# Layer-1 attention on four 32-row strips: heads in neighbouring pairs, mask and maximum in one operation

## The chip, the cores and the metric

The kernel runs on one core of a Trainium2 chip. The metric is the device time of one execution in microseconds (us), the median of several runs; before the change it is 2142.12 us, the median of three (2135.86 to 2145.12). The profile is of one more execution. A core has TensorE (PE; its weight loads are listed apart as PEld), VectorE (DVE), ScalarE (ACT), GpSimd (POOL) and SyncE (SP, which here only issues DMAs). Matmuls write to PSUM, from which DVE and ACT read.

## What is computed

Two transformer layers over 1024 tokens of width 512. Each is an attention and a feed-forward part with modulated layer norms. The change is in the attention of the second layer (layer 1 in the code), which has 32 query heads of size 16 and 8 key and value heads; four query heads share one key head. Cut to that:

```python
qkv = x @ w_qkv.T + b_qkv
q, k, v = split(qkv)                      # 32, 8 and 8 heads of 16
q, k = apply_rope(q), apply_rope(k)
k, v = repeat(k, 4, axis=1), repeat(v, 4, axis=1)
scores = einsum('bhqd,bhkd->bhqk', q, k) / sqrt(16)
scores = where(causal, scores, -1e20)
attn = softmax(scores, axis=-1)
out = einsum('bhqk,bhkd->bhqd', attn, v)
return out @ w_o.T + b_o
```

All data are float32.

## The kernel before

The attention of layer 1 begins at L530. `kT1` holds the keys, transposed, as 128 rows for each of the 8 key heads: the 16 values of the head stand four times, at rows 0, 32, 64 and 96, and row 16 of each such strip of 32 rows is one, the other 15 are zero. The queries stand in the same way, one of the four query heads of the group on each strip, with row 16 free for the (negative) maximum of the query's scores, so that the matmul itself subtracts the maximum. Before the change there are two such query tiles, `qT1[0]` and `qT1[1]`: `par` is one on the strips of even (odd) heads and zero on the others, so that `qT1[0]` holds heads 0 and 2 with zeros on the strips of 1 and 3, and `qT1[1]` the other way round. A matmul then takes a half of 64 rows, of which one strip is not zero.

The loop over token tiles `t` (L590 on) computes q, k and v (L596), rotates them on DVE and POOL (L617 to L624), transposes q and k on PE (L636) and evicts them: k with `evict`, which alternates between ACT and DVE (L78, L80), q once on DVE with the one mask (L640) and once on ACT with the other (L643).

Then come 16 units: `Q` is the half of the queries (512), `g` the key head; units 0 to 7 are Q=0, 8 to 15 Q=1. For each unit:

- `maxima_steps` (queries on the partitions): for each 128 queries `i`, each 512 keys `c` and each `pair` of heads, two matmuls into one two-bank PSUM tile `sc` (L678), the causal mask added on the diagonal block (L685, DVE, in place), and the maximum over the keys (L688, DVE). 8 such steps for a unit of Q=0, 16 for one of Q=1.
- `maxima_rows`: the negative maximum (L702, DVE), four transposes (L705), and the result added into row 16 of both query tiles (L708, DVE, twice).
- `probs_steps` (keys on the partitions): for each block of 128 keys `kb` and each pair two matmuls (L722) into `sc`, the mask on diagonal blocks (L729, DVE), and the exponential (L733, ACT) into `pr`. 8 steps for Q=0, 16 for Q=1.
- `context`: four matmuls, one per head, that accumulate probabilities times values (L745); then `context_copy` (L754, ACT) and `normalize` (L762 transposes on PE, L765 and L766 on DVE).

The pool `sp` of `sc` tiles has three buffers, which the maxima and the probabilities share; they rotate in the order of the steps, so that a step waits until the step three before it has been read out. The other two PSUM banks are for transposes and for the context.

The order around it is written out by hand: the maxima of units 0 and 1 come first; then, for each unit `n`, its probability steps with the maxima steps of unit `n+2` spread among them. One probability step is followed by its share of maxima steps, then by `tick()`, which counts down the deferred work: the context of block `kb` is due three ticks after its second step, `maxima_rows` two ticks after a unit's end, `context_copy` four, `normalize` six; `finish_half` projects the output of a half. With one maxima step to one probability step a block of keys is queued on PE as: probabilities of pair 0, maxima of pair 0, probabilities of pair 1, maxima of pair 1, context of the block before.

## Time and profile before

| what | value |
|---|---|
| median of three runs | 2142.12 us |
| the profiled execution | 2138.97 us, of which its span is 2137.2 us |
| granted TensorE clock, mean | 0.98 |
| busy: PE, DVE, ACT, POOL | 2007.7, 1224.6, 654.5, 255.3 us |
| layer-1 attention, first maxima matmul to last context | 1612.6 to 2045 us |
| unit of Q=0, Q=0 maxima ahead (units 0 to 5) | 16.3 us |
| unit of Q=0, Q=1 maxima ahead (units 6 and 7) | 23.8 us |
| unit of Q=1, maxima ahead (units 8 to 13) | 34.0 us |
| unit of Q=1, none ahead (units 14 and 15) | 20.6 us |

How to read a profile line: the group lines name the source line, the engine, the operation, output and input by the program's names with partitions and elements, the count, then the busy time in us and the mean of one in ns, and after the second bar the idle time of the engine just before these instructions and who ended it. A line of windows gives a stretch, its length, and busy time and count for each engine, then the granted TensorE clock (1.00 is full), the DMA share and GB/s. A timeline line gives the start, the duration, the engine, the line and operation, the count merged into it, and in brackets how long the engine had been idle and who released it ("issue": nothing that the profile shows).

A float32 matmul appears as two records in the trace, each with its own weight load. The durations of matmul records include the latency of the pipeline; the starts tell the pace.

### The profile page before, as it was taken

The numbers are of one execution on the slowest core, as the hardware profiler recorded it, in microseconds if no ns is written. First come the engines' busy times: TensorE is split into PE (matmuls) and PEld (weight loads), VectorE is DVE, ScalarE is ACT, GpSimd is POOL, SyncE is SP. The second block draws the span as 40 slices with busy tenths as digits, with TensorE's granted clock in tenths as the row PEclk, the third lists the DMA queues.
The fourth block names the chain that finished last, engine by engine and source line by source line (L and its number), as shares of the span: only waits on it lengthen the run. The fifth ranks groups of instructions, "written<-read, shape, count | busy, mean of one in ns | idle before, by whom it ended". The sixth has DMA issues, their size and how long they took to land.

```text
span 2137.2 us, 20442 instructions
## 1 busy us (share of the span) xinstructions
PE 2007.7 (94%) x6628; PEld 914.3 (43%) x6628; DVE 1224.6 (57%) x2305; ACT 654.5 (31%) x1180; POOL 255.3 (12%) x231
## 2 busy tenths in 40 slices
PE   5979999999999999999997999999887899999989
PEld 3434454444544445444443333333353444333344
DVE  4666656766576675766654211112477898667433
ACT  1134424434234342443532100000021323344530
POOL 0211111111111211111102000000440000000000
PEclk8999999999999999999999999999997999999999
DMA  5344334444334444343345100000300000000011
GB/s 173 103 113 134 93 104 109 110 130 100 104 97 115 127 99 114 94 111 92 90 120 167 61 30 30 0 0 0 102 0 20 1 1 1 1 1 1 1 39 40
DMA packets 87785, 151.16 MB, mean 71 GB/s; under 512 B 20896, under 2 KB 34080, under 8 KB 87680
## 3 DMA queue, kind: packets, MB, share of 16 engines
q1 hardware_dynamic: 86800, 146.98, 25.5%
q0 software_dynamic: 880, 2.88, 0.4%
q8 instruction: 54, 0.88, 0.2%
q14 instruction: 51, 0.42, 0.1%
HBM read 72.18 MB, written 2.10 MB: 35 GB/s over the span
## 4 chain that ended last, share of the span: by engine, by line
PE 72%; DVE 12%; DMA 5%; ACT 4%; issue 3%; SPq 2%; POOL 1%; DVEq 0%; POOLq 0%; ACTq 0%
PE mm L233 12%; PE mm L363 8%; PE pgu L493 7%; PE sc L319 7%; PE mm L352 6%; PE sc L722 5%; PE sc L678 5%; PE mm L519 4%; PE ctx L745 3%; DMA os<-in_s_o_dram 2%; PE pgu L497 2%; DVE mx L688 2%; DVE nb L326 2%; SPq L343 2%; DVE pr L341 1%
## 5 line engine op out<-in xcount | busy, mean ns | idle before, releaser
L329 ACT ACTIVATE pr<-sc,nb 128x1024 f32<-128x1024 f32 (+7 forms) x256 | 187.6, 735 | 386.8 <-DVE nb L326 307.4
L233 PE MATMUL mm<-hT,wf 128*128 128x512 f32 x640 | 283.2, 596 | 5.8 <-ACT wf L250 5.8
L352 PE MATMUL mm<-pT,v 128*128 128x512 f32 x576 | 263.6, 603 | 19.9 <-DMA pT<-pr 19.1
L319 PE MATMUL sc<-kT,qT 128*128 128x512 f32 (+3 forms) x768 | 273.7, 487 | 4.5 <-ACT pr L329 4.5
L363 PE MATMUL mm<-wo,ctxT 128*128 128x512 f32 x512 | 236.0, 599 | 16.4 <-ACT ctxT L358 12.0
L733 ACT ACTIVATE pr<-sc 128x1024 f32<-128x1024 f32 (+1 forms) x192 | 153.8, 810 | 236.2 <-DVE sc L729 164.8
L319 PEld LDWEIGHTS sc<-kT,qT 128*128 128x128 f32 x768 | 139.6, 191 | 154.1 <-issue 127.5
L335 ACT ACTIVATE pr<-pr,rs 128x1024 f32<-128x1024 f32 (+7 forms) x256 | 187.2, 768 | 49.1 <-DVE rs L334 48.9
L688 DVE TENSOR_REDUCE mx<-sc 128x2 f32<-128x1024 f32 (+2 forms) x192 | 182.3, 955 | 30.1 <-PE sc L678 26.7
L341 DVE STREAM_TRANSPOSE pr<-pr 128x1024 f32<-128x1024 f32 (+7 forms) x256 | 178.2, 748 | 24.0 <-ACT pr L335 18.4
L326 DVE TENSOR_REDUCE nb<-sc 128x1 f32<-128x1024 f32 (+7 forms) x256 | 188.1, 750 | 3.6
L233 PEld LDWEIGHTS mm<-hT,wf 128*128 128x128 f32 x640 | 122.2, 192 | 156.0 <-issue 147.2
L678 PE MATMUL sc<-kT,qT 64*128 64x512 f32 (+3 forms) x768 | 168.2, 520 | 13.4 <-DVE mx L688 5.2
L722 PE MATMUL sc<-qT,kT 64*128 64x512 f32 (+3 forms) x768 | 170.6, 517 | 5.4 <-DVE mx L688 3.5
L352 PEld LDWEIGHTS mm<-pT,v 128*128 128x128 f32 x576 | 110.3, 194 | 144.9 <-issue 130.1
L493 PE MATMUL pgu<-hT,gu 128*128 128x512 f32 x352 | 162.8, 606 | 0.0
L369 POOL TENSOR_TENSOR x<-x,ot 128x512 f32<-128x512 f32 x64 | 81.4, 1271 | 676.0 <-DVE ot L368 565.7
L363 PEld LDWEIGHTS mm<-wo,ctxT 128*128 128x128 f32 x512 | 94.3, 190 | 132.3 <-issue 94.2
L334 DVE RECIPROCAL rs<-rs 128x1 f32<-128x1 f32 x256 | 37.9, 156 | 125.7 <-ACT pr L329 124.6
L722 PEld LDWEIGHTS sc<-qT,kT 64*128 64x128 f32 x768 | 66.3, 187 | 101.6 <-issue 55.3
L678 PEld LDWEIGHTS sc<-kT,qT 64*128 64x128 f32 x768 | 70.0, 194 | 91.5 <-ACT pr L733 35.4
L243 POOL TENSOR_TENSOR qT<-t,t 128x512 f32<-128x512 f32 x64 | 85.5, 1336 | 182.6 <-DVE t L242 182.6
(160 smaller groups left out, 1856.1 us busy)
## 6 DMA issues: line engine op xcount, KB each, us to landing
pT<-pr SPq DMA_DIRECT2D x128, 128.0 KB, 2.4
pT<-pr SPq DMA_DIRECT2D x128, 112.0 KB, 2.3
wm<-in_wmod_dram SPq DMA_DIRECT2D x48, 256.0 KB, 3.2
pT<-pr SPq DMA_DIRECT2D x128, 96.0 KB, 2.1
pT<-pr SPq DMA_DIRECT2D x128, 80.0 KB, 2.1
wi<-in_qw_q_dram SPq DMA_DIRECT2D x32, 256.0 KB, 2.9
ws<-in_s_q_dram SPq DMA_DIRECT2D x32, 256.0 KB, 3.6
oi<-in_qw_o_dram SPq DMA_DIRECT2D x32, 256.0 KB, 2.8
```

Of the source, the lines that this page charges most:

```text
L233: nc.tensor.matmul(ps, lhsT=wf[:, c, :], rhs=hT[half][:, c, :], start=(c == 0), stop=(c == NC - 1),)
L319: nc.tensor.matmul(ps[:, n0 : n0 + w], lhsT=qT[u.g * REP + r][:, bass.ts(u.qi, P)], rhs=kT[u.g][:, n0 : n0 + w], start=True, stop=True,)
L326: nc.vector.tensor_reduce(nb, ps[:, :nk], AX.X, ALU.max, negate=True)
L329: nc.scalar.activation(pr.rearrange("p b k i -> p k b i"), ps[:, :nk].rearrange("p (k b i) -> p k b i", b=NB, i=B), AF.Exp, bias=nb, accum ...
L335: nc.scalar.activation(pr, pr, AF.Copy, scale=rs)
L341: nc.vector.transpose(t, t)
L352: nc.tensor.matmul(ps, lhsT=vv[u.g][:, kj, :], rhs=u.pT[:, :, :, kj, :].rearrange("p a r i -> p r a i"), start=(kj == 0), stop=(kj == u.n ...
L363: nc.tensor.matmul(ps, lhsT=u.ctxT[:, r, :], rhs=wo[u.g][:, r, :], start=(r == 0), stop=(r == REP - 1),)
L493: nc.tensor.matmul(ps, lhsT=gu[:, c, m, :], rhs=hT[b][:, c, :], start=(c == 0), stop=False)
L678: nc.tensor.matmul(ps[:, j, :w], lhsT=qT1[pair][kp, u.g, bass.ts(qi, P)], rhs=kT1[kp, u.g, n0 : n0 + w], start=True, stop=True,)
L688: nc.vector.tensor_reduce(u.mx[:, i, pair::2, c], ps[:, :, :w], AX.X, ALU.max)
L722: nc.tensor.matmul(ps[:, j, :w], lhsT=kT1[kp, u.g, bass.ts(kb, P)], rhs=qT1[pair][kp, u.g, u.Q * QW + q0 : (u.Q + 1) * QW], start=True, st ...
```

## The change

The two query tiles become one, `qT1`, without `par`; its eviction goes through `evict`. A step takes two heads that stand next to each other (0 and 1, or 2 and 3), each matmul on its own strip of 32 rows, so that a pair uses strips 0 and 1 or 2 and 3. On the maxima steps whose keys reach the diagonal, two `tensor_tensor_reduce` replace mask and maximum: each adds a mask row `cwide` (zeros, and the causal mask in its last 128 columns) to one head's scores, writes the sum to a scratch tile `sm` and its maximum to `mx`. `maxima_rows` adds into one tile instead of two. The order of the queue changes: after the first probability step of a block comes a tick, then all maxima steps due in the block, then the second probability step and the second tick; the maxima steps come with pair 1 before pair 0. `context` takes the heads from their new places.

```diff
-        qT1 = [hp.tile([P, NKV, S], F32, tag=f"qT1{i}", name=f"qT1{i}") for i in range(2)]
-        par = hp.tile([P, 2], F32, tag="par", name="par")
-        nc.vector.memset(par, 0.0)
-        for r in range(REP):
-            nc.vector.memset(par[32 * r : 32 * r + 32, r % 2 : r % 2 + 1], 1.0)
+        qT1 = hp.tile([P, NKV, S], F32, tag="qT1", name="qT1")
...
+        cwide = hp.tile([P, 512], F32, tag="cwide", name="cwide")
+        nc.gpsimd.memset(cwide[:, : 3 * P], 0.0)
+        nc.gpsimd.tensor_copy(cwide[:, 3 * P :], cmask)
...
-                    if src is kf:
-                        evict(kT1[:, g0 : g0 + 4, bass.ts(t, P)], ps)
-                    else:
-                        nc.vector.tensor_scalar(
-                            qT1[0][:, g0 : g0 + 4, bass.ts(t, P)], ps, par[:, 0:1], None, ALU.mult
-                        )
-                        nc.scalar.activation(
-                            qT1[1][:, g0 : g0 + 4, bass.ts(t, P)], ps, AF.Copy, scale=par[:, 1:2]
-                        )
+                    dst = kT1 if src is kf else qT1
+                    evict(dst[:, g0 : g0 + 4, bass.ts(t, P)], ps)
...
                 for j in range(2):
-                    kp = slice(64 * j, 64 * j + 64)
+                    r = 2 * pair + j
+                    kp = slice(32 * r, 32 * r + 32)
                     nc.tensor.matmul(
-                        ps[:, j, :w], lhsT=qT1[pair][kp, u.g, bass.ts(qi, P)],
+                        ps[:, j, :w], lhsT=qT1[kp, u.g, bass.ts(qi, P)],
                         rhs=kT1[kp, u.g, n0 : n0 + w], start=True, stop=True,
                     )
-                d0 = qi * P - n0
-                if d0 < 512:
-                    dg = ps[:, :, d0 : d0 + P]
-                    nc.vector.tensor_tensor(
-                        dg, dg, cmask.unsqueeze(1).to_broadcast([P, 2, P]), ALU.add
-                    )
-                nc.vector.tensor_reduce(
-                    u.mx[:, i, pair::2, c], ps[:, :, :w], AX.X, ALU.max
-                )
+                if n0 + w < (qi + 1) * P:
+                    nc.vector.tensor_reduce(
+                        u.mx[:, i, 2 * pair : 2 * pair + 2, c], ps[:, :, :w], AX.X, ALU.max
+                    )
+                    return
+                for j in range(2):
+                    r = 2 * pair + j
+                    sm = wk.tile([P, 512], F32, tag="sm", name="sm", bufs=1)
+                    nc.vector.tensor_tensor_reduce(
+                        sm[:, :w], ps[:, j, :w], cwide[:, 512 - w :], 1.0, -3e38,
+                        ALU.add, ALU.max, accum_out=u.mx[:, i, r, c : c + 1],
+                    )
...
-                for p in range(2)
+                for p in (1, 0)
...
-            for pair in range(2):
-                q = qT1[pair][:, u.g, bass.ts(u.Q, QW)]
-                nc.vector.scalar_tensor_tensor(
-                    q, ps.rearrange("p i q -> p (i q)"), par[:, pair : pair + 1], q,
-                    ALU.mult, ALU.add,
-                )
+            q = qT1[:, u.g, bass.ts(u.Q, QW)]
+            nc.vector.tensor_tensor(q, ps.rearrange("p i q -> p (i q)"), q, ALU.add)
...
                 for j in range(2):
-                    kp = slice(64 * j, 64 * j + 64)
+                    r = 2 * pair + j
+                    kp = slice(32 * r, 32 * r + 32)
                     nc.tensor.matmul(
                         ps[:, j, :w], lhsT=kT1[kp, u.g, bass.ts(kb, P)],
-                        rhs=qT1[pair][kp, u.g, u.Q * QW + q0 : (u.Q + 1) * QW],
+                        rhs=qT1[kp, u.g, u.Q * QW + q0 : (u.Q + 1) * QW],
                         start=True, stop=True,
                     )
...
-                    rhs=prs[r % 2][:, r // 2, : QW - q0], start=(kb == 0), stop=(kb == u.nkb - 1),
+                    rhs=prs[r // 2][:, r % 2, : QW - q0], start=(kb == 0), stop=(kb == u.nkb - 1),
...
             done = 0
-            for i, (kb, pair, s) in enumerate(bsteps):
-                s()
-                if pair == 1:
-                    later(3, lambda u=u, kb=kb: context(u, kb))
-                want = (i + 1) * len(asteps) // len(bsteps)
+            for i in range(0, len(bsteps), 2):
+                kb = bsteps[i][0]
+                want = (i + 2) * len(asteps) // len(bsteps)
+                bsteps[i][2]()
+                tick()
                 while done < want:
                     asteps[done]()
                     done += 1
+                bsteps[i + 1][2]()
+                later(3, lambda u=u, kb=kb: context(u, kb))
                 tick()
```

## The prediction

> **What bounds the kernel now.** I read first the table of the costliest groups, to see what the edited lines own:

> ```profile
> L733 ACT ACTIVATE pr<-sc 128x1024 f32<-128x1024 f32 (+1 forms) x192 | 153.8, 810 | 236.2 <-DVE sc L729 164.8
> L688 DVE TENSOR_REDUCE mx<-sc 128x2 f32<-128x1024 f32 (+2 forms) x192 | 182.3, 955 | 30.1 <-PE sc L678 26.7
> L678 PE MATMUL sc<-kT,qT 64*128 64x512 f32 (+3 forms) x768 | 168.2, 520 | 13.4 <-DVE mx L688 5.2
> L722 PE MATMUL sc<-qT,kT 64*128 64x512 f32 (+3 forms) x768 | 170.6, 517 | 5.4 <-DVE mx L688 3.5
> ```

> The two score matmuls have 339 us of busy PE and the maxima 182 us of DVE, all of it between 1612 and 2045 us. Half of 339 would be a large prize, so I then asked who is busy in each part of that stretch. The rows are: the first two units' maxima; one unit of Q=0 with Q=0 maxima ahead; one of Q=0 with Q=1 maxima ahead; one of Q=1 with maxima ahead; one of Q=1 without.

> ```profile
> core 0: us, PE busy (x) PEld busy (x) DVE busy (x) ACT busy (x) POOL busy (x), PEclk, DMA share, GB/s
> 1612.63:1637.20 24.57, 20.04 (x85) 9.99 (x86) 21.71 (x41) 2.09 (x2) 0.00 (x0) 0.78 0.12 43
> 1717.48:1733.80 16.32, 14.66 (x108) 6.79 (x105) 14.36 (x30) 6.10 (x9) 0.00 (x0) 1.00 0.00 1
> 1757.50:1781.34 23.84, 22.54 (x140) 9.53 (x136) 23.13 (x38) 6.10 (x9) 0.00 (x0) 1.00 0.00 1
> 1935.69:1969.68 33.99, 33.40 (x204) 12.98 (x200) 24.56 (x38) 14.40 (x17) 0.00 (x0) 1.00 0.00 1
> 2003.33:2023.98 20.65, 20.65 (x140) 7.45 (x137) 7.28 (x16) 12.90 (x16) 0.00 (x0) 1.00 0.00 1
> ```

> DVE sets the first and third (88 and 97%), PE the last two (98 and 100%), and the second is tight on both. Last I read the timeline of one block of 128 keys (the second of a Q=1 unit), to see what PE waits for:

> ```profile
> 1940.53 0.30 PEld L722 LDWEIGHTS sc<-qT,kT 64*128 64x128 f32 x4 [0.17 <-issue]
> 1940.53 1.13 PE L722 MATMUL sc<-qT,kT 64*128 64x512 f32 x4
> 1941.77 2.10 ACT L733 ACTIVATE pr<-sc 128x1024 f32<-128x1024 f32 x2 [1.10 <-PE sc L722]
> 1942.84 0.30 PEld L678 LDWEIGHTS sc<-kT,qT 64*128 64x128 f32 x4 [0.93 <-ACT pr L733]
> 1943.26 0.16 PEld L745 LDWEIGHTS ctx<-pr,v 128*32 128x32 f32 x8
> 1943.26 1.07 PE L745 MATMUL ctx<-pr,v 128*32 128x512 f32 x8
> 1944.26 0.30 PEld L722 LDWEIGHTS sc<-qT,kT 64*128 64x128 f32 x4 [0.84 <-issue]
> ```

> Three score buffers rotate, so the fourth score step of a block waits for the exponential of the first: it loads 2.31 us after the block began, behind 0.27 of latency and 1.02 of exponential. Call this the buffer loop. The change speeds none of its parts except where two steps overlap.

> **The matmuls.** A step of width 512 is 0.53 for a first pass after another mode and 0.43 for each further pass (starts 1940.53, 1941.49, 1941.71: half of it is the narrow step), 0.96 alone and 0.86 in a row. Do steps on different strips run together? One place in the trace has it, when the two halves of a step fell apart:

> ```profile
> 1636.38 1.03 PE L722 MATMUL sc<-qT,kT 64*128 64x512 f32 x1
> 1636.38 0.62 PE L678 MATMUL sc<-kT,qT 64*128 64x128 f32 x2
> ```

> Two different steps start at once on different halves. So I let neighbours overlap. But order and buffers now decide. The block was p0, m, p1, m, context (p: probabilities, m: maxima); it becomes p0, m, m, p1, context. Before, the fourth step, held by p0's exponential, was an m; now it is p1. What was overlapped ahead of it does not shorten the block; only the width of the fourth step changes, and p1 can no longer run in the shadow of p0's exponential. A block of the new Q=1 unit is 2.31 (2.78 with the mask of L729, 0.42 plus 0.05) to the fourth step, then 1.06, 0.84, 0.63 or 0.42 for width 512, 384, 256, 128 (load to next load, 1942.84 to 1943.26 is the 0.42), 0.59 for the four transposes where they fall, and the context: 1.00, 0.79, 0.57 or 0.36 by width. For narrow masked blocks the first term is 2.29, 1.87 and 1.65. In block 7, four fused operations of 0.6 keep p1's mask waiting and hold the next block's p0 exponential 0.65 to 0.85 late. The eight blocks, before (starts of L722's loads) and worked out: 4.84 to 5.2, 3.73 to 4.37, 5.21 to 4.96, 3.94 to 4.37, 4.84 to 4.84, 4.54 to 4.13, 3.77 to 3.28, 3.12 to 2.77. Sum 34.0 to 33.9. Six such units: **1 us** gained, not the 60 that halving would suggest.

> The last two units have only p0, p1, context: the two steps side by side take 0.96 where they took 1.82, so PE needs 1.96 a full block instead of 2.92. Two exponentials need 1.94 and the loop context, step, latency, exponential puts full blocks near 2.3; the masked ones I put at 2.6, 2.3, 1.8, 1.3 (before 2.91, 2.49, 1.84, 1.22). With 0.3 for the transposes 17.5 against 20.65: **6 us** for two units (4 if the loop binds throughout, 9 if never).

> **Mask and maximum.** Per unit eight L685 start 0.46 before their reductions and eight diagonal L688 follow each other 0.09 under their durations (0.33, 0.61, 0.87, 1.13, twice each): 8 x 0.45 + 2 x 2.94 = 9.5 us of DVE go. Sixteen fused operations of 128, 256, 384, 512 elements come. The trace has none. From below, a plain two-source operation out of PSUM (L787, 128x512) is 0.69, or 0.61 start to start: 6.5 a unit. From above, the addition and the maximum one after the other at 0.69 each: 1.22 start to start, 13.0 a unit. I take the row nearest in operands, L708 with two tensors and a scalar, 0.74 or 0.66 start to start (a pair is 1.41), less 1.04 ns per element (L688: 800 ns over 768): 4 x (0.26 + 0.39 + 0.53 + 0.66) = 7.4. L708 itself becomes one operation for two: 0.7 less. So 2.8 us of DVE leave each unit with maxima.

> Where DVE sets the pace this is time: 2 x 2.8 less a little for PE's clock (0.78 there) is **4.5** in the first stretch, and **5** in units 6 and 7. In units 0 to 5 the loop sets most of it. Laying a unit out as above with DVE in its queue's order (p0's mask, four fused operations, p1's mask) gives blocks of 5.35, 4.13, 3.87, 2.42 against 4.56, 4.38, 4.14, 3.25: 15.8 against 16.3, **3 us** for six. Behind p1's mask stand its exponential and the context after next; the late one is block 0.

> **The rest.** The eviction of q: L640 and L643 become copies like L78 and L80 (0.59, 0.69 for 0.75, 0.69), one for each half where there were two. PE's matmuls and the L617 chain set those 9 us steps, so only the last tile gains, **1 us**. The extra memset and copy on POOL cost under 0.54 + 0.29 (L549, L601), at 1513, where POOL then waits 18 us for a DMA; uncovered they would cost 0.8. No DMA is added. Deferred work ticks as often as before; a projection may now fall between p0 and the maxima: nothing, since PE runs it anyway.

> **Sum.** 1 + 6 + 4.5 + 5 + 3 + 1 = 20.5 from 2139.0 (the profiled execution, span 2137.2), 3 us under the median of the three runs. That is 2118.5, or 2121.6 on the median: **2120**.

> [...]

> **Rivals.** *Four strips pay in full* (12%): the queue's order turns out so that buffers don't bind. PE of a Q=1 unit falls to 34 - 11 = 23, DVE to 21.8; with some coupling 25.5, and Q=0 units 12.9: 87 us less, 2051. For it: PE at 98%. Against: the loop's waits.

> *Clock* (20%): the units of Q=0 keep PE less busy. In the first stretch, at 82% busy, the granted clock was 0.78; at 90% it was 1.00. At 0.78, some 2.5 us of matmul in a block's loop take 0.7 longer, over 24 blocks 17 us: 2135. That steps don't overlap at all lands near it too (the 6 us go: 2126).

> *The fused operation costs two passes* (16%): at 13.0 a unit DVE gains 2.9 a unit where I count a loss of 2.8. The first stretch and units 6 and 7 lose 6 each, units 0 to 5 about 10 and the Q=1 units 11 through the delayed exponentials; less 7 from the other terms, 2164. It decides above 10 us a unit, 0.9 us for 512 elements. Against: every two-source row here takes one element per 1.04 ns.

> My forecast has 52%, with 2105 to 2130 as its own range. A measurement tells about 0.5% (11 us) from no change. Nearly all of the first case and of the four strips is faster: 0.60; the clock case and the edges are within: 0.20; two passes and what the buffer order may cost beyond my layout: 0.20. The range is 2082 to 2158.

> **What would show it.** Right: L678 waiting for nothing, but L722 loads released by L733 about 2.3 us into each block; Q=1 units still near 34 us while PE's busy share falls; the last units near 17.5; a fused operation of 0.74 for 512 elements; DVE busy 2.8 less a unit. Wrong: Q=1 units under 31 (four strips), clock under 0.9 between 1640 and 1740, a fused operation over 0.9, or a DVE queue in another order than the program's.

## The result, and the profile after

The changed kernel takes 2144.21 us (median of 20 runs, 2134.24 to 2154.24), the kernel before 2141.41 beside it: a ratio of 1.0009, 95% interval 0.9995 to 1.0022. That is no change that can be told; 2120 had been forecast. The profiled execution of the changed kernel took 2141.03 us (span 2139.2, before 2137.2). Its line numbers are 7 lower in this part: L671 for L678 (maxima), L683 for the fused operation, L715 for L722 (probabilities), L726 for L733 (exponentials).

The table of the costliest groups gives busy time and mean of one, then the idle time before them and what ended it:

```profile
L726 ACT ACTIVATE pr<-sc 128x1024 f32<-128x1024 f32 (+1 forms) x192 | 152.7, 810 | 232.4 <-DVE sc L722 167.3
L715 PE MATMUL sc<-qT,kT 32*128 32x512 f32 (+3 forms) x768 | 177.5, 566 | 22.8 <-ACT pr L726 19.8
L671 PE MATMUL sc<-kT,qT 32*128 32x512 f32 (+3 forms) x768 | 158.1, 580 | 13.6 <-ACT pr L726 9.8
L683 DVE CUSTOM_DVE_ANT_0 sm<-sc,cwide 128x128 f32<-128x128 f32 (+3 forms) x256 | 125.1, 489 | 28.9 <-PE sc L715 8.4
```

The score matmuls now wait for the exponentials: before, L722 had 5.4 us of idle time ahead of it, mostly ended by DVE; L715 has 22.8, of which 19.8 were ended by L726. The mean of one is longer (566 ns for 517), a first hint that something slows them.

The rows of windows show more: first the maxima of units 0 and 1 with the start of unit 0 (about the stretch that had 24.57 us and a clock of 0.78), then units 1 to 7, one of Q=1 (unit 11) and unit 14.

```profile
core 0: us, PE busy (x) PEld busy (x) DVE busy (x) ACT busy (x) POOL busy (x), PEclk, DMA share, GB/s
1615.53:1638.15 22.62, 19.49 (x80) 9.45 (x81) 17.14 (x68) 0.71 (x1) 0.00 (x0) 0.55 0.15 46
1654.15:1670.55 16.40, 14.99 (x106) 5.89 (x104) 12.18 (x44) 6.11 (x9) 0.00 (x0) 0.90 0.00 1
1670.55:1685.75 15.20, 13.37 (x104) 5.30 (x105) 12.12 (x44) 6.11 (x9) 0.00 (x0) 1.00 0.01 2
1685.75:1704.47 18.72, 17.57 (x104) 6.86 (x104) 12.22 (x44) 6.11 (x9) 0.00 (x0) 0.73 0.00 0
1704.47:1719.67 15.20, 13.37 (x105) 5.31 (x105) 12.12 (x44) 6.11 (x9) 0.00 (x0) 1.00 0.01 1
1719.67:1739.80 20.13, 18.80 (x104) 7.31 (x104) 12.41 (x44) 6.11 (x9) 0.00 (x0) 0.66 0.00 1
1739.80:1767.93 28.13, 26.06 (x136) 10.01 (x137) 21.33 (x52) 6.22 (x9) 0.00 (x0) 0.76 0.00 1
1767.93:1791.16 23.23, 20.82 (x137) 7.92 (x137) 21.09 (x52) 6.22 (x9) 0.00 (x0) 1.00 0.00 1
1910.44:1943.92 33.48, 30.42 (x201) 10.33 (x200) 21.75 (x52) 14.08 (x17) 0.00 (x0) 1.00 0.00 1
2010.89:2029.18 18.29, 17.81 (x138) 6.04 (x137) 6.46 (x17) 13.53 (x17) 0.00 (x0) 1.00 0.00 1
```

Read the column PEclk beside the length. Units of the same work take 15.20 us at full clock, 18.72 at 0.73 and 20.13 at 0.66; before, units 1 to 5 took 16.2 to 16.3 each, all at 1.00. The units gained 1.1 us each at full clock, and those in which the clock fell paid it back, and more. DVE's busy time is 12.1 to 12.4 in all of them: it isn't DVE that stretches. Nor was PE much less busy: 13.37 of 15.20 us in unit 2 is 88%, and before it was 90%.

Cut by parts, from the first maxima load to the start of the last context matmuls the attention took 431.7 us before and 430.7 after:

| part | before | after | difference | forecast |
|---|---|---|---|---|
| first maxima and unit 0 | 39.7 | 38.6 | -1.1 | -5.0 |
| units 1 to 5 | 81.5 | 85.7 | +4.2 | -2.5 |
| units 6 and 7 | 47.5 | 51.4 | +3.8 | -5 |
| units 8 to 13 | 222.0 | 219.7 | -2.3 | -1 |
| units 14 and 15 | 41.0 | 35.3 | -5.7 | -6 |

(The forecast's 3 us for units 0 to 5 are put here as 0.5 a unit.) Two lengths given for the kernel before hold for fewer units than its table says. Unit 0 took 20.8 us at a clock of 0.84, not 16.3. Units 8 to 10 took 35.4, 46.1 and 39.2 us, not 34.0, and 35.8, 44.8 and 38.7 after the change; the projection of the first half falls there. So 34.0 stands for units 11 to 13 (33.65, 33.99, 33.65).

The attention began 2.9 us later (1615.5 us instead of 1612.6), which is why the span is 2 us longer although the attention is 1 us shorter. In the profiles of the eleven experiments it began between 1612.1 and 1619.0, so these 2.9 us are no finding, and the 1 us expected from the eviction of q can't be told.

### The profile page after: what moved, and what is told of

It is laid out like the page before. It is cut to its first block, busy times and chain, and to the rows that moved or that the text cites. A ratio compares the mean times of both kernels' runs of the same rounds, so it can differ in the third digit from the quotient of the medians.

```text
span 2139.2 us, 20527 instructions
## 1 busy us (share of the span) xinstructions
PE 1992.0 (93%) x6628; PEld 890.5 (42%) x6628; DVE 1183.5 (55%) x2532; ACT 647.0 (30%) x1172; POOL 256.8 (12%) x233
## 3 DMA queue, kind: packets, MB, share of 16 engines
q1 hardware_dynamic: 86800, 146.98, 25.5%
## 4 chain that ended last, share of the span: by engine, by line
PE 72%; DVE 12%; ACT 5%; DMA 5%; issue 3%; SPq 2%; POOL 1%; DVEq 0%; POOLq 0%; ACTq 0%
PE mm L233 12%; PE mm L363 9%; PE pgu L493 7%; PE sc L319 7%; PE mm L352 7%; PE sc L715 6%; PE mm L519 4%; PE ctx L738 3%; PE sc L671 2%; DMA os<-in_s_o_dram 2%; PE pgu L497 2%; ACT pr L726 2%; PE mm L122 2%; DVE sm L683 2%; SPq L343 2%
## 5 line engine op out<-in xcount | busy, mean ns | idle before, releaser
L726 ACT ACTIVATE pr<-sc 128x1024 f32<-128x1024 f32 (+1 forms) x192 | 152.7, 810 | 232.4 <-DVE sc L722 167.3
L715 PE MATMUL sc<-qT,kT 32*128 32x512 f32 (+3 forms) x768 | 177.5, 566 | 22.8 <-ACT pr L726 19.8
L341 DVE STREAM_TRANSPOSE pr<-pr 128x1024 f32<-128x1024 f32 (+7 forms) x256 | 178.2, 748 | 24.0 <-ACT pr L335 16.3
L671 PE MATMUL sc<-kT,qT 32*128 32x512 f32 (+3 forms) x768 | 158.1, 580 | 13.6 <-ACT pr L726 9.8
L369 POOL TENSOR_TENSOR x<-x,ot 128x512 f32<-128x512 f32 x64 | 81.5, 1273 | 676.9 <-DVE ot L368 566.7
L683 DVE CUSTOM_DVE_ANT_0 sm<-sc,cwide 128x128 f32<-128x128 f32 (+3 forms) x256 | 125.1, 489 | 28.9 <-PE sc L715 8.4
L715 PEld LDWEIGHTS sc<-qT,kT 32*128 32x128 f32 x768 | 59.4, 193 | 137.1 <-ACT pr L726 61.0
L493 PEld LDWEIGHTS pgu<-hT,gu 128*128 128x128 f32 x352 | 63.2, 189 | 96.6 <-issue 96.6
```

The lines of the kernel that those rows point to most:

```text
L341: nc.vector.transpose(t, t)
L493: nc.tensor.matmul(ps, lhsT=gu[:, c, m, :], rhs=hT[b][:, c, :], start=(c == 0), stop=False)
L671: nc.tensor.matmul(ps[:, j, :w], lhsT=qT1[kp, u.g, bass.ts(qi, P)], rhs=kT1[kp, u.g, n0 : n0 + w], start=True, stop=True,)
L715: nc.tensor.matmul(ps[:, j, :w], lhsT=kT1[kp, u.g, bass.ts(kb, P)], rhs=qT1[kp, u.g, u.Q * QW + q0 : (u.Q + 1) * QW], start=True, stop=True,)
L726: nc.scalar.activation(pr[:, :, :w], ps[:, :, :w], AF.Exp, scale=SC1)
```

## The experiments

The theory to test: the granted clock eats the gain, and it falls because a matmul on a strip of 32 rows takes up a quarter of the array (32*128 on its profile line; the largest matmuls have 128*128). Rivals: PE is merely less busy (as the forecast's clock case had it), the fused operation relieves DVE so much that PE idles, or the new order of the queue costs what the strips gain. The first four expectations (theory C) still put the fall down to idle time of PE; the share of the array came in as theory K after them. Every length of a unit below is from the start of its first probability load to that of the next unit, in one profiled execution; ratios are to the kernel before on the same chip, with 95% intervals. Each diff shows the main lines of the edit, against the changed kernel; three dots stand for the lines between.

### Only the fused operation

The kernel before with L683's operation; heads on halves of 64 rows and the old order stay:

```diff
-                    r = 2 * pair + j
-                    kp = slice(32 * r, 32 * r + 32)
+                    kp = slice(64 * j, 64 * j + 64)
...
-                        ps[:, j, :w], lhsT=qT1[kp, u.g, bass.ts(qi, P)],
+                        ps[:, j, :w], lhsT=qT1[pair][kp, u.g, bass.ts(qi, P)],
...
-            for i in range(0, len(bsteps), 2):
+            for i, (kb, pair, s) in enumerate(bsteps):
```

> The kernel before with the fused mask and maximum alone. Theory C: DVE loses 1 to 1.5 us a unit (fused operations 0.33, 0.46, 0.6, 0.73 with their accumulator reads, 8.5 a unit against 9.5), PE has the work of before, so the clock stays near 1.00 in units 0 to 7; Q=0 units 15.6 to 16.2, units 6 and 7 22 to 23, Q=1 units 34.0; total 4 to 9 us under before. Rival F (the fused operation gives nothing or costs): Q=0 units 16.3 or more, total equal to before or over it. If the clock falls here too, it is DVE's relief alone that lets it fall.

0.9972 (0.9958 to 0.9985). Windows of this kernel: first maxima with unit 0, unit 2, units 6 and 7, unit 11.

```profile
1615.88:1651.77 35.89, 30.53 (x160) 14.65 (x160) 28.26 (x106) 6.92 (x9) 0.00 (x0) 0.85 0.09 30
1667.41:1683.05 15.64, 14.55 (x108) 6.72 (x104) 12.71 (x45) 6.12 (x9) 0.00 (x0) 1.00 0.01 2
1729.97:1753.36 23.39, 22.29 (x140) 9.55 (x137) 21.65 (x53) 6.11 (x9) 0.00 (x0) 1.00 0.00 1
1753.36:1776.85 23.49, 22.20 (x140) 9.55 (x136) 21.59 (x53) 6.11 (x9) 0.00 (x0) 1.00 0.00 1
1896.74:1930.14 33.40, 33.16 (x204) 12.94 (x201) 22.73 (x53) 14.42 (x17) 0.00 (x0) 1.00 0.00 1
```

This part alone gains 6 us in the median. In the profile the attention is 9.4 us shorter, and begins 3.3 us later: it gains 3.8 in the first row (35.9 for 39.7), 0.6 to 0.7 in each of units 1 to 5, 0.7 in units 6 and 7 together, and 0.2 to 0.6 in each of units 11 to 13. The clock is 1.00 after the start, though DVE is relieved of most of what the changed kernel takes from it (12.71 us a unit for 14.36; 12.12 there).

### Only the strips, with the fused operation, in the old order

```diff
-                for p in (1, 0)
+                for p in range(2)
...
-            for i in range(0, len(bsteps), 2):
+            for i, (kb, pair, s) in enumerate(bsteps):
+                s()
...
+                want = (i + 1) * len(asteps) // len(bsteps)
```

> The changed kernel with the order of before put back (p0, m0, p1, m1 and pair 0 first). Theory C: Q=1 units 32.5 to 33.5 (the fourth step is a maximum again, and narrow in the odd blocks: block 1 at 3.73, block 3 at 3.94 where the changed order has 4.35 and 4.37; wide blocks keep 4.84), the last two units about 18.3 as in the changed kernel, since their order is the same; total 3 to 8 us under the changed kernel, with clock drops still there in units 0 to 7. Rival O: the order loses more than that, Q=1 units under 32 and total over 12 us less. Third possibility: overlap needs the alternating order, Q=1 units back at 34.0, total as the changed kernel or up to 5 us more.

1.0018 (1.0002 to 1.0033). It has the queue order of the kernel just shown, and its fused operation; the strips alone differ, with what one query tile brings instead of two: its eviction, and one addition for two in `maxima_rows`. Its first maxima with unit 0, unit 2, units 6 and 7:

```profile
1612.08:1650.13 38.05, 34.73 (x160) 15.42 (x160) 26.98 (x104) 6.92 (x9) 0.00 (x0) 0.60 0.08 28
1665.46:1680.70 15.24, 13.30 (x108) 5.67 (x104) 12.11 (x44) 6.11 (x9) 0.00 (x0) 1.00 0.01 2
1726.43:1755.66 29.23, 25.50 (x140) 10.00 (x136) 21.86 (x53) 6.11 (x9) 0.00 (x0) 0.74 0.00 1
1755.66:1789.75 34.09, 31.70 (x141) 12.48 (x137) 21.51 (x53) 6.22 (x9) 0.00 (x0) 0.55 0.00 1
```

At full clock the strips win 0.4 us a unit of Q=0 (15.24 for 15.64) and 0.5 of Q=1 (32.94 for 33.40), and 6.9 on the last two units. Then units 6 and 7 lose 16.4 us at 0.74 and 0.55, and units 8 and 10 ran at 0.89 and 0.96. So the fall is not the new order's. The gain of 3 to 8 us on the changed kernel did not come. In units 1 to 5 this kernel kept full clock on strips as well, so strips alone don't bring the fall in every unit.

### The changed kernel without the fused operation

```diff
-                    nc.vector.tensor_tensor_reduce(
...
+                d0 = qi * P - n0
+                if d0 < 512:
+                    dg = ps[:, :, d0 : d0 + P]
+                    nc.vector.tensor_tensor(
+                        dg, dg, cmask.unsqueeze(1).to_broadcast([P, 2, P]), ALU.add
+                    )
```

> The changed kernel with mask and maximum as two operations again. Theory C: DVE is back at 14 us a Q=0 unit with PE less busy than before, so the clock falls at least as long as in the changed kernel; Q=0 units 16 to 17 at full clock and 19 to 21 at half; Q=1 units 33.5 to 34.5 since the buffer loop sets them; total 5 to 15 us over the changed kernel. Rival F: total within 3 us of the changed kernel or under it.

1.0028 (1.0017 to 1.0039). Units 1 to 5 take 16.8, 19.0, 20.4, 19.6 and 17.3 us at clocks of 0.90, 0.73, 0.66, 0.74 and 0.90. Unit 2:

```profile
1671.78:1690.79 19.01, 16.98 (x104) 7.30 (x104) 13.63 (x29) 6.00 (x9) 0.00 (x0) 0.73 0.01 2
```

DVE has 13.6 us of work a unit again (14.4 before, 12.1 in the changed kernel), and the clock still falls. The kernel with the fused operation alone has less, 12.7, and its clock stays. So the relief of DVE is not the cause.

### Extra matmuls, of three kinds

If PE's idle time were the cause, any matmul in it would help; if it is the share of the array, only large ones. First a matmul of 128 rows, 128 columns and width 512 per block of units 0 to 7 and per two first maxima steps:

```diff
+        def filler(g):
+            ps = psum_tr()
+            nc.tensor.matmul(
+                ps.rearrange("p i q -> p (i q)"), lhsT=kT1[:, g, :P], rhs=kT1[:, g, :512],
+                start=True, stop=True,
+            )
...
+                if u.Q == 0:
+                    filler(u.g)
```

> The changed kernel with one extra 128x512 matmul (kT1 by kT1 into a transpose bank, read by nobody) in each block of units 0 to 7 and after every second of the first maxima steps. Theory C (the clock): the change leaves PE idle in units 0 to 7, the granted clock is 0.5 for 72 of the 140 us from 1617 to 1757 (before: 14 us from 1616), and that costs about 15 us. Then here the clock is 0.97 or more in units 0 to 7, a Q=0 unit is 15.2 to 16.0 us in spite of 3.4 us of added PE work, units 6 and 7 are 23 to 24.5, and the whole is 4 to 12 us under the changed kernel. Rival O (the queue's order is what costs, the clock follows): the added work only lengthens the units, Q=0 units 16.5 or more at full clock, total 5 to 20 us over the changed kernel.

1.0036 (1.0024 to 1.0048): units 1 to 7 run at 1.00, but at 17.3 to 17.6 us in each of units 1 to 5 (15.2 to 16.0 was expected) the filler costs more than it saves. So a smaller one, of width 256 and in the blocks alone:

```diff
+                ps[:, 0:2, :].rearrange("p i q -> p (i q)"), lhsT=kT1[:, g, :P],
+                rhs=kT1[:, g, :256], start=True, stop=True,
```

> The changed kernel with one extra 128x256 matmul, read by nobody, in each block of units 0 to 7 (none in the first maxima). Theory K (the granted clock goes by how much of the array streams: rows x columns in use x time, in windows of 3.4 us; falls under about 0.4 were followed by half clock): the changed kernel has about 0.38 in units 1 to 5, the filler adds 0.43 us of a full array per 3.8 us block, 0.11, so units 1 to 7 run at 1.00; Q=0 units 15.6 to 16.6, units 6 and 7 23.2 to 24.2; total 0 to 8 us under the changed kernel. Rival B (the clock goes by PE's busy time): the same direction. If the clock still drops in units 2 to 7, K's size is wrong. If the clock is full and the total is not under the changed kernel, the price of the clock was smaller than the 15 us read from the unit lengths.

1.0020 (1.0003 to 1.0036); units 1 to 7 run at 1.00. (The expectation's 0.38 for the changed kernel's share is 0.47 by the measure of the last section.) And the same width on a corner of 32 rows and 32 columns:

```diff
+                ps[:32, 0:2, :].rearrange("p i q -> p (i q)"), lhsT=kT1[:32, g, :32],
+                rhs=kT1[:32, g, :256], start=True, stop=True,
```

> The changed kernel with the filler of the earlier run (one matmul over 256 columns per block of units 0 to 7), but on 32 rows and 32 columns of the array instead of 128 by 128: as long, a sixteenth of the array. Theory K (the clock goes by the share of the array that streams): 0.007 more instead of 0.11, so the granted clock drops in units 1 to 7 as in the changed kernel, 20 us or more at half there, mean clock of units 1 to 7 under 0.95. Rival B (busy time decides): as with the full filler, 1.00 in units 1 to 7 and Q=0 units 16.3.

1.0170 (1.0143 to 1.0198). The pair sets busy time against the array. Units 1, 2 and 4 with the whole array's filler, and then units 1, 2, 3 and 7 with the corner's:

```profile
1662.42:1678.33 15.91, 15.45 (x116) 6.59 (x113) 12.00 (x43) 6.12 (x9) 0.00 (x0) 1.00 0.00 1
1678.33:1694.60 16.27, 15.80 (x116) 6.59 (x112) 12.21 (x45) 6.12 (x9) 0.00 (x0) 1.00 0.01 2
1710.87:1727.15 16.28, 15.81 (x116) 6.59 (x113) 12.23 (x45) 6.12 (x9) 0.00 (x0) 1.00 0.01 1
```

```profile
1655.84:1671.62 15.78, 15.31 (x116) 5.92 (x112) 11.98 (x43) 6.12 (x9) 0.00 (x0) 1.00 0.00 1
1671.62:1693.06 21.44, 21.17 (x116) 7.90 (x112) 11.94 (x45) 6.12 (x9) 0.00 (x0) 0.68 0.01 1
1693.06:1716.37 23.31, 22.79 (x116) 8.44 (x112) 12.65 (x45) 6.12 (x9) 0.00 (x0) 0.63 0.00 1
1779.26:1811.52 32.26, 31.73 (x148) 11.59 (x144) 21.62 (x53) 6.12 (x9) 0.00 (x0) 0.68 0.00 1
```

The first row of each is the same unit, 97% of it PE busy, 116 matmul records, within 0.13 us of each other. One kernel stays at 1.00, the other falls to 0.68 in the next unit. What differs is how much of the array the filler, with its weight load, takes up: 128 rows by 128 columns, or 32 by 32. The times of all executions differ as the profiles do: 2137 to 2151 us with the one filler, 2160 to 2184 with the other. Rows and columns were changed together, so the pair does not say which of them counts.

The whole array's filler brings the clock back but is itself 0.7 to 1.1 us a unit (15.91 to 16.28 for 15.20): units 1 to 7 take 129.0 us, as many as before the change. So it keeps the clock at 1.00 but is no remedy.

### Only the new order, on halves, with the fused operation

```diff
-                    kp = slice(32 * r, 32 * r + 32)
+                    kp = slice(64 * j, 64 * j + 64)
...
-            q = qT1[:, u.g, bass.ts(u.Q, QW)]
-            nc.vector.tensor_tensor(q, ps.rearrange("p i q -> p (i q)"), q, ALU.add)
+            for pair in range(2):
+                q = qT1[pair][:, u.g, bass.ts(u.Q, QW)]
```

> The kernel before with the fused operation and the new order of the queue, without the strips: the changed kernel with 64-row halves. Theory K: clock 1.00 in units 1 to 13. Theory L: the fourth step of a block is p1 and waits for p0's exponential, so the Q=1 blocks with a narrow maximum go from 3.7 to 4.4 and from 3.9 to 4.4 as in the changed kernel, wide ones are bound by PE at 4.8; Q=1 units 34 to 35; Q=0 units 15.3 to 16.5; last two as before, 20.5; total 2 to 10 us over the run with the fused operation alone. If Q=1 units stay at 33.4, the order costs nothing there.

1.0044 (1.0028 to 1.0060). Units 2, 6 and 11:

```profile
1670.61:1686.42 15.81, 14.58 (x108) 6.58 (x104) 12.81 (x45) 6.11 (x9) 0.00 (x0) 1.00 0.01 2
1733.86:1757.86 24.00, 22.48 (x141) 9.43 (x137) 21.77 (x53) 6.22 (x9) 0.00 (x0) 1.00 0.00 1
1905.24:1940.40 35.16, 34.37 (x204) 13.15 (x200) 22.44 (x54) 14.09 (x17) 0.00 (x0) 1.00 0.00 1
```

From unit 1 on the clock stays at 1.00, so neither order makes it fall. But the order itself costs 1.8 us a unit of Q=1 (35.16 for 33.40) and 0.1 to 0.6 in each of units 1 to 7. On strips it costs 0.5 (33.48 for 32.94): the order is a loss in both, and a smaller one on strips. Put the other way, the strips gain 0.5 us a unit of Q=1 in the old order and 1.7 in the new one.

### Can it be had? Context in the wait, and strips for Q=1 only

In the buffer loop, p1 waits for p0's exponential behind two maxima. If p0 and p1 are queued first, with the context between p1 and the maxima, the context fills the wait:

```diff
+                bsteps[i + 1][2]()
+                later(3, lambda u=u, kb=kb: context(u, kb))
...
-                bsteps[i + 1][2]()
-                later(3, lambda u=u, kb=kb: context(u, kb))
```

> The changed kernel with the queue p0, p1, context of the block before, m1, m0 (context_copy two ticks after a unit's end instead of four). Theory L (the buffer loop sets Q=1 units: first step, exponential, fourth step, context, one after the other): the context now fills the wait for the first exponential and the two p run side by side, so a full block goes from 4.37 to 3.5 to 4.0 and a Q=1 unit from 33.5 to 28 to 31; units 0 to 5 at full clock 13.5 to 15, but with longer times at half clock; total 10 to 30 us under the changed kernel. Rival P (PE's own work or the DVE sets Q=1 units): 33 or more, total within 5 us of the changed kernel.

1.0041 (1.0016 to 1.0067). Unit 12 takes 31.76 us at full clock (33.48 in the changed kernel), but here the clock falls in units of Q=1 as well: unit 10 took 51.63 us at 0.69 (38.65 in the changed kernel). The total expected, 10 to 30 us under the changed kernel, did not come, and 31.76 is just over the 28 to 31 expected. Twelve executions fell into two groups, six at 2139.4 to 2141.3 us and six at 2155.8 to 2160.6, so the ratio stands for neither; the profiled one is of the second. What decides which was not followed.

So the strips were kept for Q=1 alone: Q=0 has the two masked query tiles on halves and the old order throughout.

```diff
+        qT0 = [hp.tile([P, NKV, S // 2], F32, tag=f"qT0{i}", name=f"qT0{i}") for i in range(2)]
...
+            if u.Q:
+                r = 2 * pair + j
+                return r, slice(32 * r, 32 * r + 32), qT1
+            return pair + 2 * j, slice(64 * j, 64 * j + 64), qT0[pair]
...
-            for i in range(0, len(bsteps), 2):
+            for i, (kb, pair, s) in enumerate(bsteps):
```

> Units of Q=0 with the 64-row halves and masked copies of before, units of Q=1 with 32-row strips; the order of before everywhere, fused mask and maximum everywhere. Theory K: the clock in units 0 to 5 stays at 1.00 as in the run with the fused operation alone (units 15.6); in units 6 and 7, whose probabilities are on halves and whose maxima are on strips, it stays at or above 0.9 where the run with the order of before had 0.74 and 0.55; Q=1 units 32.9 and the last two 17.1 as there; total 8 to 12 us under the run with the fused operation alone, 13 to 18 under before. Rival B (busy time decides): clock drops in units 6 and 7 as with strips everywhere, since the timing of the blocks is the same, units 6 and 7 together over 55 us.

0.9941 (0.9927 to 0.9954), 2128.05 us. Units 1 to 5 are back at 15.64 and 1.00. Units 6 and 7, whose maxima ahead are Q=1's and so on strips, still ran at 0.87 and 0.93 (26.8 and 25.8 us, 5.7 more than the 46.9 of the fused operation alone). That is 13 us under the kernel before, the low end of what was expected, and unit 6 is a little under the 0.9 put as its bound.

Then both: Q=0 as there, Q=1 with the context in the wait.

```diff
+                if u.Q == 0:
+                    half = (i + 1) * len(asteps) // len(bsteps)
...
+                else:
+                    bsteps[i][2]()
+                    bsteps[i + 1][2]()
+                    later(3, lambda u=u, kb=kb: context(u, kb))
+                    tick()
```

> As the run before it (halves for Q=0, strips for Q=1), with the queue p0, p1, context, m1, m0 in the units of Q=1. Theories K and L together: Q=1 units 28 to 31 at full clock, units 1 to 5 15.6, last two 16 to 18; total 30 to 45 us under before. If the clock drops in Q=1 units, K's bound is reached there too, since the same work is then done in less time only if the buffers allow it. Rival P: Q=1 units 33, total as the run before it.

0.9923 (0.9902 to 0.9943), 2121.48 us: the lowest median of all, though its interval overlaps with that of the run before it, and better than the two kernels compared. It is 20 us under the kernel before where 30 to 45 were expected. Units 2, 6 and 11:

```profile
1666.45:1682.09 15.64, 14.55 (x108) 6.72 (x104) 12.71 (x45) 6.11 (x9) 0.00 (x0) 1.00 0.01 2
1729.02:1754.67 25.65, 22.54 (x140) 8.44 (x136) 21.77 (x53) 6.11 (x9) 0.00 (x0) 0.93 0.00 1
1896.21:1927.98 31.77, 30.70 (x203) 10.76 (x201) 21.49 (x53) 13.65 (x17) 0.00 (x0) 1.00 0.00 1
```

In unit 11 PE is now busy for 97% of the time, so little of the wait is left to fill.

Last, that order in all units, Q=0 on halves:

```diff
+                bsteps[i][2]()
+                tick()
+                bsteps[i + 1][2]()
+                later(3, lambda u=u, kb=kb: context(u, kb))
...
-            later(4, lambda u=u: context_copy(u))
+            later(2, lambda u=u: context_copy(u))
```

> Halves for Q=0, strips for Q=1, the queue p0, p1, context, m, m in all units. Theory L: Q=0 units too lose the context from their loop: 13.5 to 15 instead of 15.6, clock at 1.00 since halves keep the array share up; units 6 and 7 22 to 24; rest as in the run with this order for Q=1 alone; total 3 to 12 us under that run. Rival D (DVE's in-order queue sets Q=0 units, and both masks now stand ahead of the maxima): 15.6 or more, total the same or up to 5 us more.

0.9989 (0.9976 to 1.0002), against expectation: units of Q=0 are slower by it (15.96 to 16.19 for 15.64), units 6 and 7 took 27.1 and 27.4 at 0.94 each, and units 8 to 10 had 0.96, 0.92 and 0.92. Rival D has the units of Q=0 right; that DVE's queue is the reason was not followed.

## Why the prediction was wrong

**The step that failed is the clock.** The sum held each Q=0 unit at full clock. The fall stood as a rival at 20%, "units of Q=0 keep PE less busy", priced at 17 us. Put full-clock lengths into the table (first maxima and unit 0 as with the fused operation alone, -3.8, an estimate; units 1 to 5 at 15.20, -5.5; units 6 and 7 at 23.2, -1.1) and with the last two rows it gives -18.4 where -1.0 was measured. The 17.4 between are the clock's: 14.6 of them in units 1 to 7 (137.0 us for 5 x 15.20 + 2 x 23.2). That the rival's price comes so near is in part luck. It spread a clock of 0.78 evenly over the 24 blocks of units 0 to 5; measured were whole steps at 0.50 in units 0, 1, 3, 5 and 6, and none in 2, 4 and 7. The chance was bad because the reason was: I let 82% of PE busy go with 0.78 and 90% with 1.00, and took the clock for a matter of busy time. Luck, too, is that the terms at full clock add up to 18.4 where 19.5 had been forecast for these parts: units 6 and 7 gave 4 less than forecast, units 1 to 5 gave 3 more. Three steps of the clock's record of the changed kernel, from the end of unit 2 into unit 3, and one stretch as long of the kernel with only the fused operation, unit 2:

```profile
1682.48:1685.89 3.41, 3.29 (x34) 1.21 (x28) 2.98 (x11) 0.98 (x2) 0.00 (x0) 1.00 0.03 7
1685.89:1689.30 3.41, 2.93 (x25) 1.23 (x25) 3.16 (x15) 1.57 (x3) 0.00 (x0) 1.00 0.01 2
1689.30:1692.71 3.41, 3.41 (x19) 1.65 (x15) 1.29 (x5) 1.34 (x2) 0.00 (x0) 0.50 0.00 0
```

```profile
1670.82:1674.23 3.41, 2.65 (x22) 1.56 (x18) 3.04 (x12) 2.15 (x3) 0.00 (x0) 1.00 0.01 2
```

2.93 us of busy PE were followed by half clock, 2.65 were not: in that kernel the clock never fell after the start. The change took each score matmul from a half of the array to a quarter (64*128 to 32*128 on the profile lines, of 128*128), and nothing in my working asked what that does to the clock.

**The buffer loop: right.** Units 11 to 13 took 33.48 us each at full clock (33.9 forecast; 33.65 to 33.99 before), the eight blocks 4.52, 4.36, 4.95, 4.36, 4.84, 4.19, 3.34 and 2.92; the first is the one that was off (5.2). Weight loads of the second block of unit 11:

```profile
1914.96 0.30 PEld L715 LDWEIGHTS sc<-qT,kT 32*128 32x128 f32 x4 [0.17 <-issue]
1915.63 0.49 PEld L671 LDWEIGHTS sc<-kT,qT 32*128 32x128 f32 x8 [0.37 <-DVE mx L676]
1916.23 0.14 PEld L738 LDWEIGHTS ctx<-pr,v 128*32 128x32 f32 x2
1917.27 0.30 PEld L715 LDWEIGHTS sc<-qT,kT 32*128 32x128 f32 x4 [0.90 <-ACT pr L726]
```

p1 loads 2.31 us after p0, released by p0's exponential, as worked out. The "Four strips pay in full" rival fell: the strips' own gain in these units is 0.5 us in the old order and 1.7 in the new, not the 11 that it took off PE (half of an estimated 22: 32 score steps a unit, two passes of 0.43 us for width 512 and less for narrower ones). With another order the same strips reached 31.77 us, so the order binds; the number of buffers was not varied.

**The last two units: right**, 35.3 us for 2 x 17.5.

**Mask and maximum: right in kind, some sizes off.** The operation and its second instruction, by shape:

```profile
L683 DVE CUSTOM_DVE_ANT_0 sm<-sc,cwide 128x512 f32<-128x512 f32 x64 | 44.0, 688 | 7.6 <-PE sc L671 4.4
...
L683 DVE DVE_READ_ACCUMULATOR2_ANT mx<- 128x1 f32 x256 | 21.0, 82 | 0.0
```

0.69 for 512 elements where 0.74 was taken, but each is followed by 0.08 to read the accumulator; from start to start 0.32, 0.46, 0.59 and 0.73 for 128, 256, 384 and 512 elements, so 8.4 us a unit, not 7.4. DVE loses 2.2 us a unit (14.36 to 12.12), not 2.8. "Two passes" fell: from 128 to 512 elements the operation goes from 0.29 to 0.69 us, 1.04 ns an element. The 1.04 ns said against it of every two-source row fits L685 and L787 (0.427 us for 256 elements, 0.691 for 512), but not L623, with 1.01 and 0.88 us for 256. Of the terms other than the clock, that of units 6 and 7 was mis-sized most: 5 us forecast, 1.1 at full clock, and 0.7 with the fused operation alone. DVE was 97% busy there, but PE was 95% (22.54 of 23.84): with DVE's 2 us gone the next bound came at once. Units 1 to 5 gave 1.1 each at full clock where 0.5 was forecast.

**The new order** was priced only within the loop. It costs 0.5 us a Q=1 unit on strips, and 1.8 on halves, each against the old order.

## What to carry to other kernels

Before narrowing matmuls to strips, ask what share of the array they take up over a few microseconds, not only how busy PE is: with the two fillers above PE was 97% busy alike, and the clock was 1.00 with the one and went to 0.68 with the other; in units 3 and 5 of the changed kernel the falls cost 3.5 and 4.9 us where 1.1 had been gained. In this case strips paid where that share was higher, and halves were better where it was low: by the estimate below, units 11 to 13 of the changed kernel had 0.52 on strips (lowest step 0.40) and no fall, units 1 to 5 had 0.47 (0.35) and several. That is no safe distance, as unit 10 of the run with the context in the wait shows (a clock of 0.69). And where two engines are both nearly full, look at the second before relieving the first: in units 6 and 7, with DVE 97% and PE 95% busy, the fused operation alone took 2.9 us from DVE and gained 0.7.

## What the runs showed of the hardware

| kernel | streaming | array share, mean (lowest) | clock in units 1 to 5 |
|---|---|---|---|
| before | 0.73 | 0.70 (0.54) | 1.00 |
| fused operation only | 0.76 | 0.74 (0.59) | 1.00 |
| halves, new order | 0.75 | 0.73 (0.58) | 1.00 |
| small filler, whole array | 0.75 | 0.56 (0.39) | 1.00 |
| strips, old order | 0.70 | 0.48 (0.38) | 1.00 |
| changed kernel | 0.67 | 0.47 (0.35) | 0.66 to 1.00 |
| filler on a corner | 0.73 | 0.43 (0.27) | 0.63 to 1.00 |
| changed, not fused | 0.59 | 0.41 (0.26) | 0.66 to 0.90 |

The shares of streaming and of the array here and below are these estimates. The means don't order the clocks, the lowest steps do: strips in the old order have nearly the mean of the changed kernel and no step under 0.38. In all thirteen profiles every step ahead of a fall had an array share of 0.41 or less, while its streaming share went up to 0.76 and its share of busy PE up to 0.99. Of the steps at full clock, all 43 with a share under 0.35 were followed by half clock, 14 of the 75 between 0.35 and 0.41, and none of the 1333 above. With rows alone as the weight the two sorts don't come apart: steps of up to 0.98 then stand ahead of a fall. Full clock came back, but for three times in 70, only after steps with a share of 0.68 or more, and half clock was kept after some with up to 0.79, so that one fall costs several steps: in unit 3 of the changed kernel it lasted from 1689.3 to 1699.5 us. It is no sharp limit by this measure: between 0.35 and 0.41 most steps kept the clock. Nor did a long pause of PE come before the fall shown above: in the step ahead of it PE was busy for 2.93 of 3.41 us, so by the profile no pause was longer than 0.48 us, and by the streaming share of that step, 0.60, all pauses together came to an estimated 1.4 us.

What stays open is whether the share of the array sets the clock or only goes with it, where a limit would lie, whether rows and columns count alike, and why the same kernel's clock falls in some units and not in others of the same work. The steps' place in the work may be the reason. In the changed kernel the lightest 3.41 us between units 4 and 5 begin at 1719.4 us with a share of 0.32; a step begins at 1720.0, got 0.35, and half clock followed. Between units 3 and 4 they begin at 1704.2 and fall into two steps, of 0.39 and 0.49, and the clock stayed. No run shifted the work against the steps to test it.
